# Two-turn attention chunks, paired one-hot tables and contiguous block layout in a graph-network kernel

## The chip, the cores and the metric

The kernel runs on one core of one Trainium2 chip. The metric is device time in microseconds (us), from one launch to its end. A core has five engines that run side by side, each through its own instructions in order: PE (TensorE, the matrix products; its weight loads are listed apart as PEld), DVE (VectorE), ACT (ScalarE), POOL (GpSimd, here almost only the issuer of gathers) and SP (SyncE, here only an issuer of transfers). ACT issues transfers too. All transfers run on 16 shared DMA engines. PE writes to PSUM[...]; a pool of tiles in PSUM or SBUF hands its buffers out in turn, and an instruction that writes a tile waits until the readers of the buffer's last content are done.

## The reference

N = 32768 nodes with D = 128 features, E = 524288 edges sorted by `dst`. Two layers, cut to what matters here:

```python
# layer 0
agg = segment_sum(x[src], dst, N)                       # sum over incoming edges
h = relu((x + agg) @ W_loc1 + b) @ W_loc2 + b;  h_local = bn(x + h)
q, k, v = (x @ Wq, x @ Wk, x @ Wv) as (64 blocks, 512, 8 heads, 16)
attn = softmax(q k^T / 4);  h_attn = bn(x + (attn v) @ Wo)
h = h_local + h_attn;  out0 = bn(h + relu(h @ Wf1) @ Wf2)
x = layernorm(x + out0)
# layer 1, three steps on x
retrieved = softmax((x @ Wq.T) @ keys.T) @ values       # 512 keys
agg = zeros.at[src].add((dinv * x)[dst])                # sum over outgoing edges
x = 0.5 * x + 0.5 * (retrieved - 0.2 * (x - dinv * agg))
# at the end
x = layernorm(x1 + layernorm(x))
```

## The kernel before

The nodes are cut into 64 blocks of 512 (`BLK`), each of four chunks of 128, and into 256 windows of 128 nodes. An edge sum over a window is a chain of 19 matrix products into one PSUM tile (`seg`): each multiplies a 128x128 one-hot matrix (which edge goes to which node of the window) by 128 rows of features. Features travel as three bf16 parts side by side (`ROW` = 384 columns, 768 bytes). Twelve of the 19 row groups come from the regular exchange (`slots`, written by `spread`, read back as `y_i`), five from a list of the window's own leftover edges (`listed`, `OW` = 5), and two from a list that `GW` = 8 windows share (`common`, `SH` = 2). The last seven are gathered row by row from a table in DRAM: POOL issues one `indirect_dma_start` for each 128 rows, in `Exchange.fetch`. So each pass over the 256 windows issues 1280 gathers for `listed` and 64 for `common`.

The one-hot matrices of a window are made by one DVE operation, `Exchange.hot`: 19 x 128 comparisons per partition of a ramp with the column of the table `slot`. The ramp lies in PSUM as 32-bit numbers (`ramp_in_psum`) in two of the passes, and in SBUF as 16-bit numbers (`gc["iota1"]`) in the other two. The value of `slot` is broadcast along the innermost 128 elements.

The program runs in stages, here named by letters with their stretch in the profile:

- **A, 25 to 3529 us:** attention of layer 0, written out by hand in `attention_steps` (an order that the scheduler does not touch), with the preparation of the edge lists ("edge work": sorting networks, shifts and masks, nearly all on DVE) woven in. A *phase* is one block and one parity `o` of the heads (four heads), 128 phases in all; a phase has four chunks. In each chunk PE computes the `scores` of the *next* phase (four heads, two PSUM tiles of two heads each), small extra steps (`early`), and the `weights` products of *this* phase (again two tiles); DVE takes the row maxima of the scores (`maxima`), ACT the exponentials of the weights, and PE multiplies the exponentials of the chunk before by the values (`attend`). At the end of a phase PE transposes the maxima (`lower`), DVE adds them to the queries (`lowered`, tile `ql`, which all `weights` of the next phase read), and `half` or `whole` empties the product. The score and weight tiles come from one pool of three (`at_s`, two banks each).
  The edge work is a generator that yields the cost of what it has issued. `attention_steps` yields a boolean where edge work may be put: at the end of chunks 0 to 2 (True) and after `attend` at the phase's end (False, where work that takes a PSUM bank is not begun). At each such place the loop at the end of the program adds `SHARE` = 3.35 to a quota and issues edge work until the quota is used up.
- **B, 3529 to 4534 us:** `layer0_grid`, first part: rows of `x` are split and spread to `slots`, and the row table is written by `split_steps`.
- **C, 4534 to 6234 us:** `layer0_grid`, second part: the first pass of edge sums, order by hand, gathers asked six windows ahead.
- **D, 6234 to 6490 us:** the feed-forward part.
- **E, 6490 to 7985 us:** `layer1_grid`, first part (pool `l1p`): end of layer 0 and the first spread of layer 1. `load_tables` reads the tables `slot`, `other` and `shared` at its start.
- **F, 7985 to 12472 us:** two passes (`l1w`) in which the edge sums of one step, the retrieval and the spread of the next run together, gathers asked two windows ahead.
- **G, 12472 to 14199 us:** the last pass with the final layer norms (`l1z`), order by hand, gathers asked six windows ahead.

Between the stages, blocks of node rows go through DRAM (`part_d`, `xs_d[0]`, and the row table that the gathers read). `rows_of` writes and reads them as node rows of 128 features: within a partition the four chunks of a block lie 128 rows apart, so each run of a transfer is one row, 512 bytes (768 in the row table).

Of the kernel before, what the change touches and what calls it, by code (L numbers as in the profile page):

```python
# [32 lines left out]
GW = 8  # L33
# [3 lines left out]
SHARE = 3.35  # L37
# [373 lines left out]

class Grid:
# [130 lines left out]
    def build(self, pp):  # L543
# [9 lines left out]
        with tc.tile_pool(name="gr", bufs=1) as sp:  # L553
# [13 lines left out]
            for h in range(2):  # L567
                with tc.tile_pool(name=f"gr_h{h}", bufs=1) as hp:
# [89 lines left out]
                    with tc.tile_pool(name=f"gr_c{h}", bufs=1) as ap:  # L658
# [19 lines left out]
                        for t, n in ((0, 3), (3, OW - 3)):  # L678
# [8 lines left out]
                        nc.vector.tensor_scalar(m, lw, main.oth, P - 1, op0=OP.logical_shift_right,  # L687
                                                op1=OP.bitwise_and)
                        yield two / 3
                        nc.vector.tensor_tensor(m, m, key, OP.bitwise_or)  # L690
                        yield one / 3
# [117 lines left out]
    def build_more(self, lane, pp):  # L809
# [12 lines left out]
        with tc.tile_pool(name="mo", bufs=1) as sp:  # L822
# [10 lines left out]
            for h in range(2):  # L833
# [27 lines left out]
                nc.vector.tensor_scalar(n, word, over.oth, P - 1, op0=OP.logical_shift_right, op1=OP.bitwise_and)  # L861
                yield L / 1000
                nc.vector.tensor_tensor(m, m, n, OP.bitwise_or)
                yield L / 1000
                nc.vector.tensor_tensor(val, m, valid, OP.mult)
# [24 lines left out]
def tile_gnn_resnorm(ctx: ExitStack, tc: tile.TileContext, a: dict, out: bass.AP):  # L890
# [417 lines left out]
    def grid_consts(pool):  # L1308
# [3 lines left out]
        nc.vector.tensor_scalar(gc["lane1"], lane_f, 1.0, None, op0=OP.add)  # L1312
        gc["ident"] = pool.tile([P, P], BF16, name="ident_b")
# [5 lines left out]

    def ramp_in_psum(pool):  # L1320

        t = pool.tile([P, P], F32, name="ramp_p")
        nc.vector.tensor_copy(t, gc["iota1"])
        return t

    class Exchange:
# [16 lines left out]
        def load_tables(self, pool):  # L1343
            self.slot = pool.tile([P, NC2, NW], BF16, name="slot")
            nc.sync.dma_start(self.slot.rearrange("p c w -> p (c w)"), self.grid["slot"])
# [5 lines left out]
        def split_steps(self, wp, b, x, rest):  # L1351
# [7 lines left out]
            def end():  # L1359
                nc.vector.tensor_sub(r[:, :, 2, :], rest, r[:, :, 1, :])  # L1360
                nc.sync.dma_start(rows_of(self.table, b), t)
# [76 lines left out]
        def hot(self, wp, i, ramp, bufs):  # L1438
            oh = wp.tile([P, NC2, P], BF16, name="oh", bufs=bufs)
            nc.vector.tensor_tensor(oh, ramp[:, None, :].to_broadcast([P, NC2, P]),  # L1440
                                    self.slot[:, :, i].unsqueeze(2).to_broadcast([P, NC2, P]), OP.is_equal)
# [54 lines left out]
    def attention_steps(gp, wp, pp, p_pv, p_m):  # L1496
# [79 lines left out]
        def scores(b, o, c):  # L1576
            t = st[b]
            t["two"] = two = [pair(), pair()]
            for s in range(4):
                nc.tensor.matmul(two[s // 2][:, s % 2, :], t["q", o][32 * s:32 * s + 32, c * P:(c + 1) * P],  # L1580
                                 t["k", o][32 * s:32 * s + 32, :], start=True, stop=True)

        def maxima(b, o, c):
            m = mx[o].rearrange("p c (s z) -> p c s z", z=32)
            for i in range(2):
# [88 lines left out]
        def phase(b, o):  # L1674
# [26 lines left out]
            for c in range(NCH):  # L1701
                if n < NB:
                    yield lambda c=c: scores(n, no, c)
# [474 lines left out]
```

## Time and profile before

| | us |
|---|---|
| median of 3 runs | 14195.87 (14195.01 to 14202.4) |
| profiled execution | 14201.3 |
| its span, first to last instruction | 14199.4 |

| engine | busy us | share of the span |
|---|---|---|
| PE | 12173.8 | 86% |
| DVE | 11413.1 | 80% |
| ACT | 6658.1 | 47% |
| POOL | 6079.5 | 43% |
| DMA, all queues | 3603 MB moved | 254 GB/s |

The share over the whole span says little here, because the stages have different limits: POOL issues next to nothing before 4534 us, and the DMA engines are nearly idle during attention. So the reader needs busy time by stage. Among the costliest groups of the page are `listed` (5120 gathers, 1118 ns each on POOL), the one-hot operation (twice 512, at 2681 and 2683 ns on DVE), the row maxima (1024 at 1219 ns on DVE), the exponentials (1024 at 1023 ns on ACT), and the two products of attention: `weights` (L1602) and `scores` (L1580), listed as 4096 instructions each at about 0.7 us, which overlap one another[...].

### The profile page before, as it was taken

What the parts mean: (1) busy time and instruction counts of PE and PEld (TensorE: products, weight loads), DVE (VectorE), ACT (ScalarE), POOL (GpSimd) and SP (SyncE); (2) the same over time, 40 slices, a digit from 0 to 9 for tenths busy, and PEclk for the clock granted to TensorE, in tenths of its full rate; (3) what the DMA queues carried; (4) which work ended last, traced back from release to release, by engine and by line L of the source; (5) the groups of instructions that cost most, each with busy time, mean ns of one, the idle gap of its engine ahead of it and who ended that gap; (6) DMA issues with size and microseconds to landing.
All of it is one profiled execution on the core that took longest, in us unless ns stands there. A gap on an engine that the chain in (4) does not pass through costs nothing. (4 is left out here: it accounts for less than half of the span.)

```text
span 14199.4 us, 168166 instructions
## 1 busy us (share of the span) xinstructions
PE 12173.8 (86%) x58982; PEld 5828.9 (41%) x58982; DVE 11413.1 (80%) x16677; ACT 6658.1 (47%) x10316; POOL 6079.5 (43%) x5461
## 2 busy tenths in 40 slices
PE   8888888889887888888998799999899999966666
PEld 3232223333333444444444355555455555533333
DVE  7998998776998888877888677777677777778888
ACT  4343444334987111127888566666566666610000
POOL 0000000000001777740000477877688878767777
PEclk9898888888999999999999999999999999987787
DMA  1000000000999999977888899999999999988887
GB/s 40 11 11 17 10 11 12 18 8 33 348 346 348 309 309 309 310 242 261 304 311 308 299 383 385 390 383 383 350 376 386 382 391 381 383 292 285 286 283 256
DMA packets 1640075, 3602.99 MB, mean 254 GB/s; under 512 B 199346, under 2 KB 976466, under 8 KB 1638066
## 3 DMA queue, kind: packets, MB, share of 16 engines
q1 hardware_dynamic: 1165424, 2936.81, 55.6%
q0 software_dynamic: 258752, 533.02, 12.3%
q10 hardware_dynamic: 215042, 122.32, 2.8%
q8 instruction: 465, 7.62, 0.2%
q14 instruction: 392, 3.21, 0.1%
HBM read 2088.45 MB, written 1503.00 MB: 253 GB/s over the span
## 5 line engine op out<-in xcount | busy, mean ns | idle before, releaser
L1429 POOL DMA_INDIRECT listed<-rows,other x5120 | 5725.6, 1118 | 3544.2 <-issue 3151.1
L1416 ACT CAST y_o<-exp 128x768 bf16<-128x768 f32 x4224 | 3224.0, 808 | 1271.9 <-DMA slots<-y_o 627.2
L1411 PE MATMUL exp<-rows,pick 128*128 128x384 bf16 x12288 | 2768.2, 326 | 394.9 <-ACT y_o L1416 289.4
L1453 PEld LDWEIGHTS <-oh 128*128 128x128 bf16 x19456 | 1992.2, 102 | 2648.8 <-issue 1629.8
L1453 PE MATMUL seg<-y_i,oh 128*128 128x384 bf16 x12288 | 2745.0, 349 | 9.3 <-DMA y_i<-slots 9.3
L1416 DVE CAST y_o<-exp 128x768 bf16<-128x768 f32 x1920 | 1830.9, 954 | 687.4 <-PE exp L1411 636.2
L1411 PEld LDWEIGHTS <-pick 128*128 128x128 fp8e4 x12288 | 1185.1, 97 | 2115.5 <-issue 1550.7
L1453 PE MATMUL seg<-listed,oh 128*128 128x384 bf16 (+1 forms) x5120 | 1257.6, 336 | 815.5 <-DMA listed<-rows,other 777.2
L1606 ACT ACTIVATE pT<-s 128x1024 f32<-128x1024 f32 x1024 | 1021.5, 1023 | 1353.7 <-PE s L1602 1351.3
L1586 DVE TENSOR_REDUCE mx<-s 128x2 f32<-128x1024 f32 x1024 | 1204.4, 1219 | 270.5 <-PE s L1580 270.2
L1440 DVE TENSOR_TENSOR oh<-ramp_p,slot 128x2432 bf16<-128x2432 f32 x512 | 1372.3, 2681 | 12.7 <-DMA slot<-slot_dst 9.4
L1440 DVE TENSOR_TENSOR oh<-iota,slot 128x2432 bf16<-128x2432 bf16 x512 | 1373.7, 2683 | 3.0 <-DMA slots<-y_o 3.0
L283 POOL DMA_INDIRECT c_r<-pivots_over,c_ix x2 | 1.9, 946 | 3056.7 <-DVE c_ix L281 3056.4
L1602 PE MATMUL s<-ql,k 32*128 32x512 f32 x4096 | 1032.4, 692 | 259.2 <-DVE mx L1586 244.6
L2005 DVE SCALAR_TENSOR_TENSOR part_i<-seg,dinv,part_i 128x128 f32<-128x128 f32 x1536 | 529.6, 345 | 543.0 <-PE seg L1453 531.9
L1064 ACT ACTIVATE ln_rs<-ln_mv,eps_c 128x4 f32<-128x4 f32 x192 | 57.1, 297 | 1670.8 <-DVE ln_mv L1062 1489.7
L1930 PE MATMUL s<-keysT,qT 128*128 128x512 f32 x1536 | 818.2, 615 | 7.3 <-ACT pr L1043 3.7
L1453 PE MATMUL seg<-common,oh 128*128 128x384 bf16 (+1 forms) x2048 | 600.7, 350 | 194.5 <-DMA common<-rows,shared 194.2
L1942 PE MATMUL s<-pt,values 128*128 128x512 f32 x1536 | 750.6, 600 | 10.8 <-ACT pt L1937 10.6
L1580 PE MATMUL s<-k,q 32*128 32x512 f32 x4096 | 745.2, 726 | 6.0 <-DVE mx L1586 2.6
L1613 PE MATMUL pv<-pT,vx 128*32 128x512 f32 x4096 | 698.6, 751 | 0.2 <-ACT pT L1606 0.2
L1388 PE MATMUL row_p<-row,ident_b 128*128 128x512 bf16 x1536 | 601.8, 392 | 82.9 <-DVE pick L1381 62.3
(393 smaller groups left out, 14180.8 us busy)
## 6 DMA issues: line engine op xcount, KB each, us to landing
slots<-y_o SPq DMA_DIRECT2D x2048, 576.0 KB
y_i<-slots SPq DMA_DIRECT2D x1024, 1152.0 KB
pick<-pick SPq DMA_DIRECT2D x1024, 192.0 KB
listed<-rows,other POOLq DMA_INDIRECT x5120
rows<-rows SPq DMA_DIRECT2D x192, 384.0 KB
part_d<-part_o SPq DMA_DIRECT2D x192, 256.0 KB
part_i<-part_d ACTq DMA_DIRECT2D x192, 256.0 KB
rows<-rows SPq DMA_DIRECT2D x64, 386.0 KB
```

The costliest lines, as they stand in the source:

```text
L1411: nc.tensor.matmul(ps[:, j, :ROW], pick[:, o:o + P], r, start=True, stop=True)
L1416: (nc.vector.tensor_copy if to_dve else nc.scalar.copy)(dst, ps[:, :, :ROW])
L1429: nc.gpsimd.indirect_dma_start(out=g[:, k, :], out_offset=None, in_=self.table, in_offset=bass.IndirectOffsetOnAxis(ap=index[:, k:k + 1], ...
L1440: nc.vector.tensor_tensor(oh, ramp[:, None, :].to_broadcast([P, NC2, P]), self.slot[:, :, i].unsqueeze(2).to_broadcast([P, NC2, P]), OP.is ...
L1453: nc.tensor.matmul(ps[:, :n], oh[:, j, :], src, start=(k == 0), stop=(k == NC2 - 1))
L1580: nc.tensor.matmul(two[s // 2][:, s % 2, :], t["q", o][32 * s:32 * s + 32, c * P:(c + 1) * P], t["k", o][32 * s:32 * s + 32, :], start=Tru ...
L1586: nc.vector.tensor_reduce(m[:, c, 2 * i:2 * i + 2, xr[o]], st[b]["two"][i], AX.X, OP.max, negate=True)
L1602: nc.tensor.matmul(two[s // 2][:, s % 2, :], t["k", o][32 * s:32 * s + 32, c * P:(c + 1) * P], t["ql", o][32 * s:32 * s + 32, :], start=Tr ...
L1606: nc.scalar.activation(t["p", c][:, 2 * i:2 * i + 2, :], two[i], AF.Exp)
L1613: nc.tensor.matmul(t["o"][32 * s:32 * s + 32, :], t["v"][:, c, s, 2 * o:2 * o + 2, :].rearrange("p z e -> p (z e)"), t["p", c][:, s, :], s ...
L1930: nc.tensor.matmul(s, st["q"][:, c * P:(c + 1) * P], keysT, start=True, stop=True)
L1942: nc.tensor.matmul(ps, values[:, k, :], st["pt"][:, k, :], start=(k == 0), stop=(k == NCH - 1))
```

## The change

There are six parts.

1. **Attention in two turns a chunk.** `scores`, `maxima` and `weights` get an index `i` and handle two heads and one PSUM tile at a time. A turn issues the `weights` of heads 2i and 2i + 1 and then the `scores` of the other two heads of the next phase. `attend` and the `early` steps follow the first turn. A place for edge work is added after the first turn (`yield False`), so there are eight places in a phase and not four; `SHARE` goes from 3.35 to 1.65, and a yield of −n waits about as many chunks as before.
2. **`GW` from 8 to 16:** sixteen windows share the two common row groups.
3. **`slot` holds each value twice,** window first: the DVE compares pairs of neighbours, so that no operand has an innermost step of 0. `load_tables` reads the table into a temporary tile and makes the two copies on DVE, in C and again in E.
4. **The PSUM ramp** becomes bf16, made by a PE transpose.
5. **Block layout in DRAM:** `kept_of` keeps a partition's four rows next to one another, for the row table, `xs_d[0]` and `part_d`. `x` and `out` keep their layout.
6. **`row_index`:** the gather indices follow the new layout of the row table; it adds four DVE operations to each of the four places where the indices are made.

```diff
-GW = 8
+GW = 16
-SHARE = 3.35
+SHARE = 1.65
+def row_index(nc, dst, spare, window, lane):
+    n = NCH.bit_length() - 1
+    cost = dst.shape[-1] / 1000
+    lane(dst)
+    yield cost
+    nc.vector.tensor_scalar(dst, dst, n, None, op0=OP.logical_shift_left)
+    yield cost
+    nc.vector.tensor_scalar(spare, window, 7, NCH - 1, op0=OP.logical_shift_right, op1=OP.bitwise_and)
+    yield cost
+    nc.vector.tensor_tensor(dst, dst, spare, OP.bitwise_or)
+    yield cost
+    nc.vector.tensor_scalar(spare, window, 7 + n, 7 + n, op0=OP.logical_shift_right, op1=OP.logical_shift_left)
+    yield cost
+    nc.vector.tensor_tensor(dst, dst, spare, OP.bitwise_or)
+    yield cost
...
+    def kept_of(t, i):
+        return t.rearrange("(b p c) d -> b p (c d)", c=NCH, p=P)[i]
...
     def ramp_in_psum(pool):
-        t = pool.tile([P, P], F32, name="ramp_p")
-        nc.vector.tensor_copy(t, gc["iota1"])
+        t = pool.tile([P, P], BF16, name="ramp_p")
+        nc.tensor.transpose(t, gc["down"], gc["ident"])
...
         def load_tables(self, pool):
-            self.slot = pool.tile([P, NC2, NW], BF16, name="slot")
-            nc.sync.dma_start(self.slot.rearrange("p c w -> p (c w)"), self.grid["slot"])
+            self.slot = pool.tile([P, NW, NC2, 2], BF16, name="slot")
+            with tc.tile_pool(name="slot_l", bufs=1) as lp:
+                t = lp.tile([P, NC2, NW], BF16, name="slot_1")
+                nc.sync.dma_start(t.rearrange("p c w -> p (c w)"), self.grid["slot"])
+                for o in range(2):
+                    nc.vector.tensor_copy(self.slot[:, :, :, o], t.rearrange("p c w -> p w c"))
...
         def hot(self, wp, i, ramp, bufs):
-            nc.vector.tensor_tensor(oh, ramp[:, None, :].to_broadcast([P, NC2, P]),
-                                    self.slot[:, :, i].unsqueeze(2).to_broadcast([P, NC2, P]), OP.is_equal)
+            nc.vector.tensor_tensor(oh.rearrange("p c (w z) -> p c w z", z=2),
+                                    ramp.rearrange("p (w z) -> p w z", z=2)[:, None].to_broadcast([P, NC2, P // 2, 2]),
+                                    self.slot[:, i].unsqueeze(2).to_broadcast([P, NC2, P // 2, 2]), OP.is_equal)
...
-        def weights(b, o, c):
-            two = [pair(), pair()]
-            for s in range(4):
-                nc.tensor.matmul(two[s // 2][:, s % 2, :], t["k", o][32 * s:32 * s + 32, c * P:(c + 1) * P],
+        def weights(b, o, c, i):
+            ps = pair()
+            for s in (2 * i, 2 * i + 1):
+                nc.tensor.matmul(ps[:, s % 2, :], t["k", o][32 * s:32 * s + 32, c * P:(c + 1) * P],
                                 t["ql", o][32 * s:32 * s + 32, :], start=True, stop=True)
...
             for c in range(NCH):
-                if n < NB:
-                    yield lambda c=c: scores(n, no, c)
-                yield from early[c]
-                yield lambda c=c: weights(b, o, c)
-                if n < NB:
-                    yield lambda c=c: maxima(n, no, c)
-                if c:
-                    yield lambda c=c: attend(b, o, c - 1)
+                for i in range(2):
+                    yield lambda c=c, i=i: weights(b, o, c, i)
+                    if n < NB:
+                        yield lambda c=c, i=i: scores(n, no, c, 1 - i)
+                    if i == 0:
+                        if c:
+                            yield lambda c=c: attend(b, o, c - 1)
+                        yield from early[c]
+                    if n < NB:
+                        yield lambda c=c, i=i: maxima(n, no, c, 1 - i)
+                    if i == 0:
+                        yield False
                 yield from late[c]
                 if c < NCH - 1:
                     yield True
...
-                nc.sync.dma_start(rows_of(self.table, b), t)
+                nc.sync.dma_start(kept_of(self.table, b), flat(t))
...
-                    nc.sync.dma_start(rows_of(part_d, b), part)
+                    nc.sync.dma_start(kept_of(part_d, b), flat(part))
...
-                    nc.scalar.dma_start(p_i, rows_of(part_d, b))
+                    nc.scalar.dma_start(flat(p_i), kept_of(part_d, b))
...
-                        quota = (us + 1) * SHARE
+                        quota = (2 * us + 1) * SHARE
```

## The prediction

> **What bounds the kernel now.** I read busy time by stage first, because shares of the whole span mix seven different limits. The lines are the stages B, C, D, E, the two passes of F, G and A, each with the busy time of PE, weight loads, DVE, ACT and POOL, then the granted PE clock, the DMA share and GB/s.
>
> ```profile
> core 0: us, PE busy (x) PEld busy (x) DVE busy (x) ACT busy (x) POOL busy (x), PEclk, DMA share, GB/s
> 3529.00:4534.00 1005.00, 839.73 (x3840) 368.34 (x3840) 933.66 (x1289) 895.85 (x1281) 6.57 (x62) 0.99 0.91 344
> 4534.00:6234.00 1700.00, 1374.99 (x6640) 734.75 (x6640) 1497.78 (x2687) 184.73 (x445) 1270.63 (x1344) 0.93 0.93 307
> 6234.00:6490.00 256.00, 242.81 (x528) 96.79 (x528) 143.40 (x209) 135.39 (x197) 0.00 (x0) 0.96 0.59 199
> 6490.00:7985.00 1495.00, 1310.03 (x6025) 693.57 (x6026) 1266.82 (x2375) 1276.27 (x2110) 13.08 (x11) 0.99 0.85 303
> 7985.00:10205.00 2220.00, 2077.22 (x10518) 1137.58 (x10517) 1602.32 (x2094) 1329.16 (x2204) 1736.48 (x1340) 0.99 1.00 376
> 10205.00:12472.00 2267.00, 2117.35 (x10725) 1158.81 (x10722) 1623.37 (x2129) 1373.33 (x2276) 1742.98 (x1339) 0.99 1.00 376
> 12472.00:14199.00 1727.00, 1099.30 (x4864) 546.55 (x4864) 1393.19 (x2881) 39.32 (x129) 1294.97 (x1344) 0.79 0.85 282
> 25.00:3529.00 3504.00, 3108.80 (x15840) 1090.86 (x15839) 2948.37 (x2994) 1420.75 (x1670) 13.78 (x15) 0.87 0.05 15
> ```
>
> F has its DMA engines full (1.00) and PE at 94%. In C and G no engine looks full, yet POOL is. The timeline of POOL, in G and then in F, shows it:
>
> ```profile
> 13200.65 0.94 POOL L1429 DMA_INDIRECT listed<-rows,other  x1 [0.30 <-issue]
> 13201.90 0.94 POOL L1429 DMA_INDIRECT listed<-rows,other  x1 [0.30 <-issue]
> ...
> 9005.42 2.68 DVE L1440 TENSOR_TENSOR oh<-iota,slot 128x2432 bf16<-128x2432 bf16 x1
> 9005.53 3.40 POOL L1429 DMA_INDIRECT listed<-rows,other  x1 [0.30 <-issue]
> ```
>
> In G a gather starts every 1.25 us, 0.94 busy and a constant 0.30 of issue; C's 1344 gathers at 1.25 us are 1680 of its 1700 us. In F the gather that meets a one-hot operation lasts until just after it.
>
> For A I read the waits between 300 and 3000 us (total us, times, longest):
>
> ```profile
> PEld s L1602 <- DVE mx L1586: 422.8, 263, 4.4
> ...
> DVE mx L1586 <- PE s L1580: 147.7, 84, 10.4
> ...
> DVE ql L1596 <- PE m L1591: 54.3, 38, 4.3
> ...
> DVE aval L1628 <- ACT asum L1627: 40.4, 39, 1.8
> ```
>
> The first line is the second pair of weights waiting for a PSUM tile that DVE still reads. The others are DVE's own waits.
>
> The program's own cost yields, summed, give 1485 quota units, which at 3.35 are 443 of the 512 chunks; 69 chunks carry no edge work. Those are PE's: between 3400 and 3500 us PE is busy 98.6 of 100 us with 616 matmul instructions, and at 15840/512 = 30.9 instructions a chunk takes 5.0 us. The others take (3504 - 69 x 5.0)/443 = 7.13 us, 28.5 a phase. DVE works (2948 - 69 x 3.0)/443 = 6.19 us of it, 24.7 a phase (3.0 is its 60% in the free chunks). So DVE bounds A, with 3.8 us of idle a phase; the three DVE waits are 242 us over 2700/28.5 = 95 phases, 2.6 of the 3.8.
>
> [...] the 16-bit one-hot takes 2683 ns, like the 32-bit one. [...] A's clock is 0.87 and the stretch at 3400 us has 1.00.
>
> **The change part by part**, against the execution of 14201.3 us.
>
> *GW.* Each pass issues 32 gathers fewer. In C and G POOL is the limit: 32 x 1.25 = 40 us each, 80 off. I see no second limit within 2%: DVE is busy 88% in C and 81% in G and gets lighter.
>
> *One-hot.* Rows of DVE two-input operations give 1348 ns at 1152 elements and 2547 at 2304, so 1.04 ns per element and 0.15 us fixed; 2432 come to 2.68. [...] 0.15 + 1216 x 1.04 = 1.41 us. It saves 1.27 us of DVE per window, 325 us a pass, but DVE sets the end in none of C, F, G: nothing directly. In F it shortens the hold on POOL, where gathers average 1.28 us against 0.95; POOL is 1736 us busy plus 0.30 x 1340 = 402 of issue, 2138 of 2220, a near second limit that moves out of the way. The PSUM form makes no difference to the sum, as DVE has room.
>
> *Block layout and DMA in F.* A 512-byte packet: the ACT queue in F has 66000 packets at 2.5% of 16 x 4487 us, 27 ns each. A 2 KB packet: in D 24036 packets at 64.8% of 16 x 200 us, 95 ns after setting the 2672 tiny ones at nothing. So four short runs cost 109 ns, one long 95, which makes 4.5 ns of overhead a packet. Part reads, part writes and row writes each drop 3 x 8192 packets a pass: 332 us of engine time, 21 us on 16 engines. Upper value: setting E's and F's SP queue against each other (195 thousand packets, 336 MB, 86% of 16 x 1100 us; 191 thousand, 536 MB, 81.9% of 16 x 1700 us) gives 16 ns a packet for that mix, mostly writes: 62 us with the reads at a middle value. Fewer common rows: 4096 x 36 ns / 16 = 9 us. Between 30 and 71 a pass; I take 45 as the DMA engines are full all along: 90 off for F. If bytes alone count, only the 9 a pass remain. In B, E and G the same saving lies beside DVE, ACT or POOL and counts nothing.
>
> *Table load.* Two DVE copies of 4864 elements, 5.2 us each by the same slope. In C the table is now loaded during B (its transfer stands in the SP queue there), which takes away the 9.4 us for which DVE waited, and POOL runs ahead six windows: nothing. In E the order of instructions shows SP's first load of `pick` waiting for the copies, with the loads of `vT` and `x` behind it on SP; ACT, PE and DVE wait for those. The table needs about 6.9 us to land (as in C), so the first `vT` load goes out at 6490.4 + 6.9 + 10.4 + 0.9 = 6508.6 instead of 6491.8: 16 us on.
>
> *Index.* Four operations more at four places: three at 0.62 and one at 1.09 us (the rows of 896 elements), 12 us of DVE in A.
>
> *Turns in A.* The order of instructions shows weights waiting for DVE (the maxima two turns back) and scores for ACT (the exponentials of the turn before). All of PE's work in a phase at full clock is 4 x (1.14 + 1.14 + 1.06 + about 1.1) + 0.66 = 18.3 us, from the timeline. New on PE: after a chunk's second turn the next scores wait for the exponential just begun: 1.14 + 0.1 + 1.02 us after its weights start instead of 1.14, so 1.1 us, three times a phase; behind them stand `attend` and `early`. At the phase's end `lower` waits for the last maxima (1.3), and the first weights for `lowered` (0.7), with the scores behind. That is 18.3 + 5.3 = 23.6, and 18.3/0.87 + 5.3 = 26.3 at the clock of now. What DVE gains: `lower` no longer stands behind a weights pair and an `attend`, so 2.6 us of waits become about 0.9: 24.7 + 0.9 = 25.6. Two in-order engines that wait for each other end above the larger; I take the middle of 26.3 and 28.5, 27.4 us: 1.1 x 111 phases = 122 off. In chunks without edge work PE is the limit and its path grows from 20.0 to 23.6: 58 such chunks (the yields end at place 908 of 1024), 14.5 phases, 52 on. With 12 for the index: A gives 58 off. Bounds: 26.0 a phase gives 214 off; 30.4 gives 275 on.
>
> Sum: A -58, C -40, G -40, F -90, E +16, B and D 0: -212, so 13989 of 14201.3. The median stands 5.4 under that execution: **13984 us**.
>
> **Rivals.**
> 1. *DVE's idle goes almost wholly.* Phase 26.0: -214 in A, in all -368: 13828. For: most of DVE's idle is at phase ends. Against: PE's path of 26.3.
> 2. *F is limited by bytes.* -18 there: 14056. For: 376 GB/s in both passes, the most of any stage. Against: C and G have 0.93 and 0.85 shares at lower rates, so short packets do cost engine time.
> 3. *Slower: PE becomes the limit of A.* The wait for the exponential, in order, opens gaps[...]. The other parts give 154 off and A's fixed losses are 64, so it decides from (154 - 64)/111 = 0.8 us more a phase, 29.3, which is a mean clock of 18.3/(29.3 - 5.3) = 0.76. At 0.73 the phase is 30.4: A +275, in all +121: 14317. For: stretches of A stand at 0.77 to 0.79 now. Against: ACT is busy 41% in A and answers at once, while now PE waits 423 us for a loaded DVE.
> 4. *The one-hot does not get its double rate.* F keeps POOL near its limit and gets half its gain: about 14030.
>
> **Chances.** Forecast 0.48, rival 1 0.25, rival 2 0.10, rival 4 0.06, rival 3 0.09, other 0.02. A measurement of this kernel tells 0.2% (28 us) from no change. Faster 0.87, same 0.04, slower 0.09. The range, 13770 to 14170, takes in the first two cases with A's bounds, and rivals 2 and 4.
>
> **What would show it.** C and G at about 1660 and 1687 us with 1312 gathers at 1.25 us; `oh` near 1.41 us; F's passes near 2175 and 2220 with gathers near 1.1 us; `vT` of E loaded 16 us later; in A waits of scores on `pT` on PE, fewer DVE waits for `m`, a clock near 0.87 and a length near 3446 us. The prediction is wrong if A's clock falls below 0.76, if gathers in C and G get longer, or if F's DMA stays full at an unchanged length.

## The result and the profile after

The changed kernel takes 14102.55 us (median of 4 runs) where the kernel before takes 14197.09: the ratio is 0.9929, 95% interval 0.9916 to 0.9943. It is faster by 95 us; 212 were forecast, and the predicted time was 13984. The direction was right and the size was less than half.

The stages of the changed kernel, A to G in order, cut at the same events as those shown of the kernel before (columns: stretch, length, then busy time and count of PE, weight loads, DVE, ACT, POOL, then PE clock, DMA share, GB/s):

```profile
25.00:3674.00 3649.00, 2929.18 (x15840) 1063.47 (x15839) 2952.03 (x3010) 1434.22 (x1670) 13.81 (x15) 0.87 0.04 14
3674.00:4676.00 1002.00, 839.20 (x3841) 368.32 (x3841) 933.00 (x1289) 894.25 (x1281) 6.63 (x62) 0.99 0.89 347
4676.00:6342.00 1666.00, 1343.10 (x6645) 719.39 (x6646) 1217.21 (x2691) 185.10 (x445) 1246.83 (x1312) 0.95 0.93 311
6342.00:6600.00 258.00, 242.18 (x525) 95.91 (x523) 143.13 (x206) 135.61 (x197) 0.00 (x0) 0.96 0.58 197
6600.00:8109.00 1509.00, 1313.77 (x6027) 694.90 (x6028) 1273.99 (x2377) 1276.58 (x2110) 12.49 (x13) 0.98 0.83 301
8109.00:10267.00 2158.00, 2067.97 (x10628) 1156.79 (x10627) 1306.03 (x2112) 1352.76 (x2240) 1393.89 (x1328) 0.99 1.01 390
10267.00:12426.00 2159.00, 2068.51 (x10611) 1154.85 (x10610) 1303.76 (x2110) 1352.84 (x2240) 1350.71 (x1283) 0.99 1.01 389
12426.00:14116.00 1690.00, 1090.96 (x4864) 543.61 (x4864) 1074.60 (x2880) 39.32 (x129) 1266.99 (x1312) 0.80 0.84 286
```

| Stage | Before, us | After, us | Change | Forecast |
|---|---|---|---|---|
| A | 3504 | 3649 | +145 | -58 |
| B and D | 1261 | 1260 | -1 | 0 |
| C | 1700 | 1666 | -34 | -40 |
| E | 1495 | 1509 | +14 | +16 |
| F, both passes | 4487 | 4317 | -170 | -90 |
| G | 1727 | 1690 | -37 | -40 |

The forecast is right within 6 us in four rows and wrong in A and F, which err in opposite directions: A is 203 us worse than forecast, F 80 us better. A's clock is 0.87, as before, and DVE is busy for the same time (2952 against 2948 us), so neither a slower clock nor more work explains it. In F the DMA share stays full (1.00, then 1.01) while GB/s rise from 376 to 390: the same bytes cost less engine time.

For A, the waits of the changed kernel between 300 and 3000 us (total us, times, longest):

```profile
PEld m L1623 <- issue: 395.2, 95, 6.8
PE m L1623 <- DVE arec L1674: 306.3, 92, 5.8
...
DVE mx L1618 <- PE s L1613: 239.4, 138, 6.9
PEld s L1613 <- ACT pT L1638: 225.2, 273, 3.8
...
PEld s L1634 <- DVE mx L1618: 177.3, 169, 2.6
PEld s L1634 <- DVE ql L1628: 136.4, 72, 12.0
...
DVE aval L1660 <- ACT asum L1659: 65.0, 45, 1.8
...
DVE ql L1628 <- PE m L1623: 20.8, 27, 1.3
```

The wait of the weights for a PSUM tile that DVE still reads, 423 us before, is down to 177. But DVE's own wait for scores has grown from 148 to 239 us, and PE has waits that are new or far longer: 306 us of `lower` for the reciprocal (`arec`), 136 us of weights for `ql`, 225 us of scores for exponentials (`pT`). The timeline of the changed kernel around the end of one phase shows how they hang together (start, duration, engine, line; in brackets the idle time before and what ended it):

```profile
2019.86 2.35 DVE L1618 TENSOR_REDUCE mx<-s 128x2 f32<-128x1024 f32 x2
2022.12 0.25 DVE L1674 RECIPROCAL arec<-m 128x16 f32<-128x16 f32 x1
2022.29 2.49 DVE L654 TENSOR_TENSOR mask<-kept_w,moved 128x2304 int32<-128x2304 int32 x1
...
2022.52 1.09 PE L1623 MATMUL m<-ident,mx 128*128 128x128 f32 x4 [4.70 <-DVE arec L1674]
...
2024.70 0.68 DVE L1628 TENSOR_TENSOR ql<-m,q 128x512 f32<-128x512 f32 x1
...
2025.43 1.22 PE L1634 MATMUL s<-ql,k 32*128 32x512 f32 x2
...
2027.27 1.23 DVE L1618 TENSOR_REDUCE mx<-s 128x2 f32<-128x1024 f32 x1 [0.37 <-PE s L1613]
...
2041.20 0.30 PEld L1613 LDWEIGHTS s<-k,q 32*128 32x128 f32 x4 [1.35 <-ACT pT L1638]
...
2048.99 0.69 DVE L1628 TENSOR_TENSOR ql<-m,q 128x512 f32<-128x512 f32 x1 [1.27 <-PE m L1623]
...
2052.93 1.23 DVE L1618 TENSOR_REDUCE mx<-s 128x2 f32<-128x1024 f32 x1 [3.25 <-PE s L1613]
```

DVE runs the last two maxima and the reciprocal; PE, whose only other work of the phase (`attend` of the last chunk) stands behind `lower` in its order, stands 4.70 us until `lower` may start. Then DVE takes the edge work of the phase's end (`mask`, 2.49 us) ahead of `ql`. The weights of the new phase wait for `ql`, the first scores come right behind them, and DVE in turn waits for those scores: 0.37 us here, and at the end of the next phase, where no edge work is due, 1.27 us for `lower` ahead of `ql` and 3.25 us for the scores (last two lines). The line at 2041.20 is the other wait that grew: scores held 1.35 us by the exponential of the turn before.

The sizes differ along the stage. Measured from one `ql` to the next, a phase without edge work takes 19.2 to 19.9 us before and 23.9 to 24.0 after. The 82 phases from the eleventh on, called full below, take 27.55 us before and 27.78 after, with DVE busy 24.83 and 24.52 of it. The next 29, called late, go from 29.72 to 31.25 us, with DVE busy 22.8 and 22.9. The first ten and the last six, which carry less edge work or none, are called light.

In F, POOL's timeline of the changed kernel shows the gather that meets a one-hot:

```profile
9006.50 1.45 POOL L1461 DMA_INDIRECT listed<-rows,other  x1 [0.30 <-issue]
```

It lasts 1.45 us in place of the 3.40 of before; the gathers there average 1.05 us (1394 us over 1328).

### The profile page after: what moved, and what is told of

Same layout as the page of the kernel before. It is cut to its first block, busy times and chain, and to the rows that moved or that the text cites. A ratio compares the mean times of both kernels' runs of the same rounds, so it can differ in the third digit from the quotient of the medians.

```text
span 14115.9 us, 167928 instructions
## 1 busy us (share of the span) xinstructions
PE 11898.4 (84%) x58984; PEld 5798.9 (41%) x58984; DVE 10207.9 (72%) x16696; ACT 6674.0 (47%) x10316; POOL 5292.3 (37%) x5333
## 5 line engine op out<-in xcount | busy, mean ns | idle before, releaser
L1461 POOL DMA_INDIRECT listed<-rows,other x5120 | 5146.9, 1005 | 4142.6 <-issue 3147.8
L1486 PE MATMUL seg<-y_i,oh 128*128 128x384 bf16 x12288 | 2636.7, 346 | 21.7 <-DMA y_i<-slots 21.2
L1486 PE MATMUL seg<-listed,oh 128*128 128x384 bf16 (+1 forms) x5120 | 1308.1, 335 | 900.4 <-DMA listed<-rows,other 887.8
L1618 DVE TENSOR_REDUCE mx<-s 128x2 f32<-128x1024 f32 x1024 | 1243.5, 1219 | 448.4 <-PE s L1613 446.6
L1613 PE MATMUL s<-k,q 32*128 32x512 f32 x4096 | 1261.4, 698 | 65.0 <-ACT pT L1638 59.0
L1634 PE MATMUL s<-ql,k 32*128 32x512 f32 x4096 | 1213.0, 683 | 87.0 <-DVE mx L1618 60.2
L1431 DVE TENSOR_SCALAR_CACHE_REDUCE pick<-row_p,lane 128x512 fp8e4<-128x512 f32 x768 | 556.4, 746 | 256.0 <-PE row_p L1420 241.0
L1472 DVE TENSOR_TENSOR oh<-iota,slot 128x2432 bf16<-128x2432 bf16 x512 | 724.1, 1414 | 3.0 <-DMA slots<-y_o 3.0
L1472 DVE TENSOR_TENSOR oh<-ramp_p,slot 128x2432 bf16<-128x2432 bf16 x512 | 723.6, 1414 | 3.5 <-DMA slots<-y_o 3.3
L1486 PE MATMUL seg<-common,oh 128*128 128x384 bf16 (+1 forms) x2048 | 629.2, 349 | 73.4 <-DMA common<-rows,shared 73.2
```

The source lines that it names most:

```text
L1461: nc.gpsimd.indirect_dma_start(out=g[:, k, :], out_offset=None, in_=self.table, in_offset=bass.IndirectOffsetOnAxis(ap=index[:, k:k + 1], ...
L1472: nc.vector.tensor_tensor(oh.rearrange("p c (w z) -> p c w z", z=2), ramp.rearrange("p (w z) -> p w z", z=2)[:, None].to_broadcast([P, NC2 ...
L1486: nc.tensor.matmul(ps[:, :n], oh[:, j, :], src, start=(k == 0), stop=(k == NC2 - 1))
L1613: nc.tensor.matmul(ps[:, s % 2, :], t["q", o][32 * s:32 * s + 32, c * P:(c + 1) * P], t["k", o][32 * s:32 * s + 32, :], start=True, stop=True)
L1618: nc.vector.tensor_reduce(m[:, c, 2 * i:2 * i + 2, xr[o]], st[b].pop(("two", i)), AX.X, OP.max, negate=True)
L1634: nc.tensor.matmul(ps[:, s % 2, :], t["k", o][32 * s:32 * s + 32, c * P:(c + 1) * P], t["ql", o][32 * s:32 * s + 32, :], start=True, stop= ...
```

## The experiments

The kernels ran on different chips. On the one of e1 to e4 and that of e13 the kernel before takes 15095 and 15159 us, on the others 14203 and 14208. On the first of these the stages with gathers are longer (C, F and G of e1 take 1071 us more than those of e6) and A is not: the same order of attention takes 3503 us there (e1) and 3506 on another (e6); for e13's chip there is no such pair. So times are compared only on one chip, and otherwise by stage. The changed kernel itself was timed on neither of the slower chips; e3 below, which leaves its A as it was, takes 0.75% longer than the kernel before on the first, so the gain is not to be expected on every chip. In the text and the tables of this section A is counted to the first cast of the row table, 6 to 8 us more than in the cuts above: 3510 us before, 3657 after.

**e1, the old turns.** Everything of the change except the attention order and SHARE.

```diff
-SHARE = 1.65
+SHARE = 3.35
-                for i in range(2):
-                    yield lambda c=c, i=i: weights(b, o, c, i)
-                    if n < NB:
-                        yield lambda c=c, i=i: scores(n, no, c, 1 - i)
+                if n < NB:
+                    yield lambda c=c: scores(n, no, c)
+                yield from early[c]
+                yield lambda c=c: weights(b, o, c)
...
-                        quota = (2 * us + 1) * SHARE
+                        quota = (us + 1) * SHARE
```

> The changed kernel with the attention order of before (SHARE 3.35, both score tiles first in a chunk); all other parts kept. Theory 1, the two turns themselves cost A's 145 us: stage A goes from 3649 back to about 3510 (3504 plus a few us for the row index), the other stages stay, and the time is 14103 - 139 = about 13964 us (13945 to 13985). Theory 2, A grew for another reason (the index operations, the placing of the edge work around them): A stays above 3600 and the time above 14050.

Measured: A 3503 us, so the two turns, together with the places for edge work and the SHARE that belong to them, are A's whole loss, and the row index costs nothing visible. (e10 below keeps SHARE and the eight places, one of them moved, and has no loss, so their number by itself does not cost it.) The time of 15050.76 (ratio to before 0.9971, 0.996 to 0.9983) missed the expected figure because of the chip, not because of A: C, F and G together are 1071 us longer than in e6, on another chip. Stage C is

```profile
4520.00:6497.00 1977.00, 1453.93 (x6640) 745.22 (x6641) 1189.17 (x2688) 181.94 (x445) 1247.58 (x1312) 0.89 0.80 263
```

which is 311 us more than in the changed kernel above, at a DMA share of 0.80 in place of 0.93. In a run of gathers one still starts every 1.25 us, but 1312 of them make only 1640 of the 1977 us: POOL now also waits, among others 136 us for edge sums (`seg`) where it waited 30 above. Why this chip is slower was not settled.

**e2, extra steps in the second turn.** `early` moves behind the scores of the second turn; `attend` stays in the first.

```diff
-                    if i == 0:
-                        if c:
-                            yield lambda c=c: attend(b, o, c - 1)
-                        yield from early[c]
+                    if i == 0 and c:
+                        yield lambda c=c: attend(b, o, c - 1)
+                    if i == 1:
+                        yield from early[c]
```

> The changed kernel with the extra steps (early) issued in the second turn of a chunk and attend alone left in the first. Theory 1a, PE's wait for the exponential between a second turn and the next chunk's first turn sets the light phases: they fall from 24.0 us towards 21 to 21.5 (three waits of 1.1 us), waits of scores on pT in 300 to 3000 us fall from 267 us to below 120, A loses 60 to 120 us; time 13985 to 14045. Theory 1b, the end and the start of a phase set them (lower behind the last maxima and the reciprocal, scores behind ql): the light phases stay above 23 us and A moves by less than 25 us.

Measured: the first ten phases fall from 25.6 to 22.8 us, the last six from 27.4 to 25.9, the full ones rise from 27.78 to 28.06; A 3623. The waits of scores for exponentials, in all 267 us in the changed kernel (300 to 3000 us), are 139, a little above the 120 expected:

```profile
PEld s L1613 <- ACT pT L1638: 115.0, 109, 3.6
...
PE s L1613 <- ACT pT L1638: 24.1, 60, 2.7
```

The wait for the exponential is real and makes up most of the loss of the first ten phases; it is not what keeps the full ones long. The expected 60 to 120 us were 34, since the full phases gave a part back. The time was 15176.63, ratio 1.0056 (1.0037 to 1.0075).

**e3, scores first at a phase's start.**

```diff
+                    if n < NB and c == i == 0:
+                        yield lambda c=c, i=i: scores(n, no, c, 1 - i)
                     yield lambda c=c, i=i: weights(b, o, c, i)
-                    if n < NB:
+                    if n < NB and (c or i):
                         yield lambda c=c, i=i: scores(n, no, c, 1 - i)
```

> The changed kernel with the scores of the first turn of a phase issued ahead of its weights, the other seven turns unchanged. Theory 1b, DVE stands still at the start of a phase because the scores that it needs stand behind weights that wait for ql: DVE's wait for scores in 300 to 3000 us falls from 239 us to below 150, the full phases (10 to 92) fall from 27.8 us by 0.7 to 1.2, A loses 70 to 130 us; time 13970 to 14035. Theory 1a (the exponential's wait alone): A moves by less than 25 us.

Measured: A 3652, full phases 27.77, and 1.24 us of idle time ahead of the first maxima in place of 1.41; ratio 1.0075 (1.0056 to 1.0095). A miss: DVE's wait for scores was to fall below 150 us and to take 70 to 130 us off A. The scores still stand behind `lower` and `attend`, and at one phase's end in its trace `attend` ends when `ql` is done as well (2029.1 and 2029.0 us), so taking `ql` out of their way is not enough.

**e5, scores ahead of `lower`.** The first scores of the next phase and their maxima are issued before `lower` and `lowered` (`n2` is the phase after the next).

```diff
-                    if n < NB:
+                    if n < NB and c + i:
                         yield lambda c=c, i=i: scores(n, no, c, 1 - i)
...
+            if n2 < NB:
+                yield lambda: scores(n2, no2, 0, 1)
+            yield lambda: attend(b, o, NCH - 1)
             if n < NB:
                 yield lambda: lower(n, no)
-            yield lambda: attend(b, o, NCH - 1)
+            if n2 < NB:
+                yield lambda: maxima(n2, no2, 0, 1)
             yield n == NB
             if n < NB:
                 yield lambda: lowered(n, no)
```

> The changed kernel (two turns) with the first scores of the next phase, and their maxima, issued before the present phase's lower and lowered, and attend of the last chunk ahead of lower; the other seven turns unchanged. Theory 1c, in the full phases DVE stands still at the start of a phase because PE issues nothing for it until lower and attend are through: the idle time ahead of the first maxima falls from 1.4 us a phase to below 0.5, the full phases (10 to 92) from 27.8 to 26.6 to 27.1 us, and A from 3657 to between 3530 and 3590 us. Rival, the idle time only moves on to the next thing that DVE needs (ql, the sum): A stays within 25 us of 3657.

Measured: A 3798, worse by 141, so a miss; 14254.38 us, ratio 1.0038 (1.0024 to 1.0052). Its timeline says why:

```profile
2016.25 2.56 DVE L652 TENSOR_TENSOR moved<-kept_w,mask 128x2304 int32<-128x2304 int32 x1
2018.73 0.68 DVE L1628 TENSOR_TENSOR ql<-m,q 128x512 f32<-128x512 f32 x1
2019.47 0.51 PEld L1634 LDWEIGHTS s<-ql,k 32*128 32x128 f32 x4 [4.44 <-DVE ql L1628]
...
2025.67 1.23 DVE L1618 TENSOR_REDUCE mx<-s 128x2 f32<-128x1024 f32 x1 [6.25 <-PE s L1613]
```

`lower` is done at 2015.3, but DVE has edge work ahead of `ql`, which runs at 2018.73. PE stands for 4.44 us, and since the one set of maxima that was to cover this is already done, DVE then stands for 6.25.

**e9, edge work behind `ql`.** Only the place for edge work at the phase's end moves (here and in e10 and e13 the slot source is kept as in e6, which concerns E alone).

```diff
-            yield n == NB
             if n < NB:
                 yield lambda: lowered(n, no)
             yield lambda: half(b) if o == 0 else whole(b)
+            yield n == NB
```

> The changed kernel (two turns) with the edge work of a phase's end placed behind lowered and half or whole, in place of ahead of them; nothing else in A changed (and the slot source kept, as in e6). Theory 1d: weights first makes PE stand until ql is there, and ql stands on DVE behind that edge work; moved, PE's waits for ql in 300 to 3000 us fall from 154 us to below 60 and the idle time ahead of the first maxima from 1.4 us to below 0.5 a full phase; DVE in turn waits about 1.3 us for lower, so the full phases fall only by 0.3 to 1.0 us, A from 3657 to 3570 to 3630. Rival, the waits for the exponential are all of the loss: A within 20 us of 3657.

Measured: A 3700 (14139.81 us, ratio 0.9955, 0.9939 to 0.9972). The idle time ahead of the first maxima fell from 1.41 to 0.67 and PE's waits for `ql` from 154 to 82 us, neither as far as expected (below 0.5, below 60), and DVE now waits 1.25 us for `lower` ahead of `ql`, where the edge work had covered it: full phases 28.24. A miss in size and sign.

**e10 and e13, the places together.** e13 joins e5 and e9; e10 adds e2's edit.

> e10 with the extra steps left in the first turn as in the changed kernel: e5's scores ahead of lower together with e9's edge work behind ql, slot source kept. Each of these two alone made the full phases longer (29.2 and 28.2 against 27.8 us). Theory 1e, two waits follow one another at the phase's end on DVE (for lower, then for the first products behind ql), and one piece of work covers only one of them: together they bring the full phases below 27.2 us, while the light phases stay above 24 us, since the waits for the exponential remain; A between 3520 and 3580. Rival, moving the extra steps was what helped in e10: the full phases stay above 27.7 us and A above 3620.

> Two turns with e5's scores ahead of lower, e9's edge work behind ql and e2's extra steps in the second turn, slot source kept. If these three places hold the whole loss of the two turns, DVE works nearly through: full phases 26.3 to 26.8 us, light phases 21 to 22.5, A 3420 to 3480, below the 3506 of the old turns. If the turns have a further cost [...], A stays above 3520.

| Kernel | full phases, us | idle of DVE ahead of first maxima / `ql`, us a full phase | first ten phases, us | late phases, us | A, us |
|---|---|---|---|---|---|
| before | 27.55 | 0.51 / 0.53 | 22.2 | 29.7 | 3510 |
| after | 27.78 | 1.41 / 0.24 | 25.6 | 31.3 | 3657 |
| e5 | 29.23 | 2.88 / 0.07 | 24.6 | 32.4 | 3798 |
| e9 | 28.24 | 0.67 / 1.25 | 25.4 | 31.5 | 3700 |
| e13 = e5 + e9 | 27.26 | 0.92 / 0.48 | 24.8 | 30.6 | 3589 |
| e10 = e13 + e2 | 26.77 | 0.34 / 0.68 | 22.7 | 29.5 | 3487 |
| e6, old turns | 27.28 | 0.38 / 0.42 | 22.1 | 29.9 | 3506 |
| e12, old turns, edge moved | 29.60 | 0.05 / 2.65 | 22.3 | 31.5 | 3744 |

e5 and e9, each a loss alone, are together a gain of 68 us: A 3589, just outside the 3520 to 3580 expected, with full phases of 27.26 where below 27.2 was expected (15202.43 us on its chip, ratio 1.0033, 1.002 to 1.0047). Adding e2's edit brings A to 3487, a little above the expected 3420 to 3480. e10 takes 13918.18 us, ratio 0.9797 (0.978 to 0.9813), and is faster than both kernels. Its interval overlaps that of e6 below; that it is ahead of the old turns rests on A, 3487 against 3506 (e1, e6, e7, e8 and e11, all with the old turns' order, have 3503 to 3508). So with its three places mended the order of two turns is worth about 20 us, in one profiled execution. The end of a phase in e10:

```profile
2000.50 1.16 DVE L1617 TENSOR_REDUCE mx<-s 128x2 f32<-128x1024 f32 x1
...
2000.63 0.65 PE L1622 MATMUL m<-ident,mx 128*128 128x128 f32 x4 [1.64 <-DVE arec L1673]
...
2001.57 0.67 DVE L1627 TENSOR_TENSOR ql<-m,q 128x512 f32<-128x512 f32 x1
...
2002.16 1.35 DVE L660 TENSOR_SCALAR mask<-kept_w 128x2304 int32<-128x2304 int32 x1
2002.30 0.31 PEld L1633 LDWEIGHTS s<-ql,k 32*128 32x128 f32 x8 [1.25 <-DVE ql L1627]
...
2004.33 1.23 DVE L1617 TENSOR_REDUCE mx<-s 128x2 f32<-128x1024 f32 x1 [0.82 <-PE s L1612]
```

DVE's two waits of a phase's end each have a piece of work beside them: maxima (1.16 us) beside `lower`, edge work (1.35) beside the first weights. PE waits 1.25 us for `ql`, DVE 0.82 us for the next scores.

**e12, the same move in the old order.** e9's edit on e6.

> e6 (old turns) with the edge work of a phase's end behind lowered, as in e9. In the old order PE has scores to issue that need no ql, so theory 1d says that the place of the edge work matters little: A within 25 us of 3506. If the place matters by itself, A moves by as much as between the changed kernel and e9.

Measured: A 3744, worse by 238 (14178.93 us, ratio 0.9979, 0.9971 to 0.9986). A clear miss of mine: in the old order DVE needs the edge work ahead of `ql`, because `lower` stands on PE behind a pair of weights and an `attend`; without it DVE waits 2.65 us a full phase there. So theory 1d, which looked only at who waits for `ql`, falls; what fits all the cases of the table is 1e: at a phase's end DVE has a wait for `lower` and one for the first scores, and the order decides which of them has work beside it.

**e6, the slot source kept.** With the old turns, the table that the two copies read is taken from the stage's pool and not freed.

```diff
-            with tc.tile_pool(name="slot_l", bufs=1) as lp:
-                t = lp.tile([P, NC2, NW], BF16, name="slot_1")
+            t = pool.tile([P, NC2, NW], BF16, name="slot_1")
```

> Old turns as in e1, and the table that the slot copies read stays allocated, so that the first load of pick in E need not wait for the copies. If E's 14 us are that wait, E goes from 1510 back to 1494 to 1500 us and everything else stays as in e1; if they are the copies themselves on DVE, E stays above 1506. It is also the base for e7 and e8.

Measured, stages A, E and the two passes of F:

```profile
25.00:3523.00 3498.00, 3087.43 (x15840) 1081.12 (x15839) 2958.48 (x3010) 1419.46 (x1670) 13.78 (x15) 0.88 0.05 15
...
6449.00:7944.00 1495.00, 1307.50 (x6025) 692.97 (x6026) 1274.27 (x2377) 1275.65 (x2110) 11.83 (x13) 0.99 0.84 303
7944.00:10104.00 2160.00, 2070.33 (x10626) 1158.49 (x10625) 1303.23 (x2110) 1349.79 (x2238) 1392.60 (x1329) 0.99 1.01 389
10104.00:12252.00 2148.00, 2062.01 (x10616) 1153.61 (x10614) 1304.82 (x2113) 1354.04 (x2243) 1354.53 (x1284) 1.00 1.01 391
```

E is back at 1495 us (1509 in the changed kernel, 1510 in e1): its 14 us were `pick`'s wait for freed memory, and the copies cost nothing else. Time 13943.65, ratio 0.9815 (0.9798 to 0.9831).

**e7, e8, e11 and e4: which part pays in C, F and G.** Each takes one part away from e6: the paired one-hot, with the table copies and the bf16 ramp (e7), GW 16 (e8), the block layout with its index (e11). e8 frees the slot source as the changed kernel does, so its time also holds the 14 us of E; its C, F and G are not touched by that. e4 took the layout away from the changed kernel on the slower chip.

```diff
-                                    self.slot[:, i].unsqueeze(2).to_broadcast([P, NC2, P // 2, 2]), OP.is_equal)
+                                    self.slot[:, :, i].unsqueeze(2).to_broadcast([P, NC2, P]), OP.is_equal)
...
-GW = 16
+GW = 8
-                nc.sync.dma_start(kept_of(self.table, b), flat(t))
+                nc.sync.dma_start(rows_of(self.table, b), t)
...
-                    nc.sync.dma_start(kept_of(part_d, b), flat(part))
+                    nc.sync.dma_start(rows_of(part_d, b), part)
```

> Old turns with the one-hot at single rate (slot table not doubled, 32-bit ramp in PSUM), against e6. Theory 4, the slow one-hot holds POOL's gathers up and F starves for them: F grows by 30 us or more, C and G by less than 10. Theory 3, F is set by its DMA engines alone: F grows by less than 15 us. In both DVE has room in C and G.

> Old turns with GW 8 in place of 16 (32 gathers more a pass), against e6. If POOL's 1.25 us a gather sets C and G, each grows by 35 to 42 us and F by 8 to 15 a pass; if on this chip the landing of gathers sets them, C and G grow by less than 20.

> e6 (old turns, slot source kept) with the node-row layout of before and no row index. On a chip where the DMA engines are full in F, as in the runs before and after, theory 3 (12 to 16 ns a packet) gives F + 110 to 150 us against 4302; theory 4 less than 80. C, G, B and E within 10 us.

> The changed kernel with the node-row layout of before in DRAM (runs of 512 and 768 bytes) and without the row index; GW, one-hot and turns kept. Theory 3, the cost of a packet was taken too small (4.5 to 12 ns; 73728 packets a pass at 16 ns are 74 us on 16 engines): F grows from 4317 us by 130 to 150, A loses 0 to 12, time about 14225 to 14255. Theory 4, a good part of F's 170 us comes from POOL, whose gathers the faster one-hot no longer holds up: F grows by less than 100 us and the time stays below 14200.

The two passes of F without the paired one-hot (e7), then without the block layout (e11):

```profile
7939.00:10124.00 2185.00, 2085.29 (x10629) 1146.72 (x10628) 1613.49 (x2111) 1351.57 (x2240) 1731.50 (x1330) 0.99 1.00 385
10124.00:12301.00 2177.00, 2078.98 (x10611) 1143.50 (x10609) 1610.50 (x2112) 1350.97 (x2241) 1692.32 (x1283) 0.99 1.01 386
```

```profile
7952.00:10186.00 2234.00, 2086.33 (x10626) 1155.39 (x10624) 1308.98 (x2111) 1349.54 (x2240) 1391.13 (x1328) 0.99 1.01 376
10186.00:12420.00 2234.00, 2081.66 (x10613) 1152.50 (x10612) 1306.98 (x2111) 1351.03 (x2241) 1345.45 (x1283) 0.99 1.01 376
```

C and G in e6, then in e8:

```profile
4520.00:6194.00 1674.00, 1351.66 (x6649) 721.69 (x6649) 1220.00 (x2693) 186.34 (x447) 1250.23 (x1312) 0.95 0.93 311
...
12252.00:13941.00 1689.00, 1091.41 (x4864) 543.97 (x4864) 1075.12 (x2880) 39.32 (x129) 1266.78 (x1312) 0.80 0.85 286
```

```profile
4525.00:6233.00 1708.00, 1383.51 (x6650) 738.34 (x6649) 1215.27 (x2693) 186.25 (x448) 1273.66 (x1344) 0.93 0.92 306
...
12298.00:14028.00 1730.00, 1092.94 (x4864) 543.19 (x4864) 1075.09 (x2881) 39.32 (x129) 1295.07 (x1344) 0.79 0.84 281
```

Against e6's 2160 and 2148 us, e7's passes are 25 and 29 longer: 54 us for the one-hot. POOL is busy 1731 us of 2185 there, plus 0.30 us of issue for each of its 1330 gathers, 2130 in all: near the end of the pass, as before the change. Over both passes it waits 62 us there for edge sums to free a gather's tile, and 692 in e6, so its slack is nearly gone. The DMA engines are full in both (shares of 1.00 and 1.01), so how the two limits share the 54 us is not shown. e7's C and G are within 10 us of e6's. e11's are 74 and 86 longer, 160 us for the layout, at 376 GB/s, the rate of before; 110 to 150 were expected. e8's passes are 9 us shorter in sum, no more than F differs between e6 (4308) and the changed kernel (4317), so GW shows no gain in F, where 8 to 15 us a pass were expected; C and G grow by 34 and 41 us (to 1708 and 1730), POOL's 32 gathers. The parts of F sum to more than the 179 us between before and e6, as they may, since each was removed with the others in place. The times: e7 13997.03 (0.9855, 0.9839 to 0.9872), e8 14014.38 (0.9862, 0.9845 to 0.9878), e11 14129.36 (0.9947, 0.993 to 0.9963). e4's F, 4895 us on the slower chip, is only 36 to 69 longer than in e1, e2 and e3 (4826 to 4859): there the DMA share in F is 0.96 and the layout counts less. (Its A is 24 us below that of the changed kernel; e11's is 2 below e6's, so this is not put down to the index.) Its time, 15228.82 (1.0085, 1.0069 to 1.0102), does not tell theories 3 and 4 apart for the chip of the result; e7 and e11 do: both parts pay, and of theory 3's 16 ns a packet only the total comes near (below).

The DMA queue that SP fills, over F, first in e11, then in e6 (packets, MB, share of 16 engines):

```profile
q1 hardware_dynamic: 494131, 1388.02, 80.9%
```

```profile
q1 hardware_dynamic: 395941, 1387.92, 81.8%
```

On queue 1, 98190 packets fewer save 0.809 x 16 x 4468 - 0.818 x 16 x 4308 = 1451 us of engine time. It would be wrong to divide the one by the other (14.8 ns each), because most of the queue's packets are the same in both. Sorted by size, the packets of the two traces took, in us of all 16 engines together:

| Packets in F | e11 | e6 |
|---|---|---|
| writes of `part_d`, 512 bytes or 2 KB | 112 (27.4 ns each) | 86 (84.6 ns each) |
| writes of the row table, 768 bytes or 3 KB | 148 (36.1 ns) | 125 (121.8 ns) |
| reads of `part_d`, 512 bytes or 2 KB | 109 (27.4 ns) | 87 (87.2 ns) |
| the rest of SP's queue, mostly 4608 bytes, unchanged | 3354 (187.4 ns at 4608 bytes) | 3314 (185.2 ns) |
| gathers, unchanged | 756 | 732 |

The packets that the layout changed save 71 us, about 8 ns for each packet that is gone, writes and reads alike. Another 65 us lie in packets that it did not change and that became a little shorter. The stretch is 160 us shorter; the last 24 were not settled, nor why the unchanged packets became shorter.

## Why the prediction was wrong

- **C and G, right.** 80 us forecast, 71 measured, with 1312 gathers still at 1.25 us. e8 gives the gain back, 75 us.
- **One-hot, right in its duration, wrong in its worth.** 1.41 us was forecast and 1.414 measured, with the ramp in PSUM (1414 ns) and in SBUF (1415 ns) alike. That pairs would halve the 1.04 ns per element of the trace was the author's estimate, which nothing in the kernel before showed. "Nothing directly" was wrong: POOL, "a near second limit that moves out of the way", was given no price, and e7 shows 54 us for the one-hot in F.
- **Layout, mis-sized.** Of the 45 us a pass 36 were for the layout, 72 for both, between the lower value of "4.5 ns of overhead a packet" and the upper one of 16. The packets that the layout changed did save 71. That the middle came out so is chance: the 95 ns of a 2 KB packet, read in D, were 84.6 to 87.2 in F, so the lower value should have been 7 to 8 ns, and the upper one had its 16 ns from a mix of packets, while those on SP's queue cost no more than those on ACT's (27.4 ns each at 512 bytes). The step that failed is that the layout saves these packets' own time and nothing else: e11 shows 160 us for it. Packets of unchanged size became shorter too, 65 us, which no term of the sum had; the last 24 are open.
- **GW in F, wrong.** 18 us were forecast for fewer common rows; e8 shows no gain.
- **Table load, right.** +16 forecast, +14 measured; e6 shows the mechanism, memory freed after the copies (E 1495 us where it is kept).
- **Index, too dear.** 12 us forecast in A; with it A is 3506 us in e6 and without it 3504 in e11.
- **A, wrong in sign.** PE's side held: clock 0.87, path of a phase without edge work 23.6 us forecast and 24.0 measured, waits for the exponential where they were expected. The step that failed is DVE's, "2.6 us of waits become about 0.9". Between 300 and 3000 us the three waits counted there were 242 us before and are 325 after (239 for scores, 65 for `aval`, 21 for `lower`), 3.4 us over each of the same 95 phases. The part that was argued came true, the wait for `lower` fell; but I priced the wait of the first weights for `lowered` at 0.7 us, the duration of that operation, and left out the edge work standing ahead of it on DVE, and DVE's own wait for the scores that now stand behind those weights. e9 shows that moving the edge work alone does not help; e13 and e10 show that covering both waits does. In the full phases the gain of 1.1 us became a loss of 0.23, in the late ones a loss of 1.53: 82 x 0.23 + 29 x 1.53 = 63 us in place of -122. The light phases cost 33 us in the first ten and 47 in the last six, 80 against 52 forecast; edge work now reaches into the last six (DVE busy 17.4 us a phase, 11.9 before).
- **The mean behind A's sum.** 28.5 us a phase with 3.8 us of DVE idle mixes two kinds of phase. The full ones had 2.7 us of idle before, the late ones 6.9. In the late ones DVE's wait for scores was 83 us over the 29 phases before and is 160 after, and 60 us before were steps of the sorting networks (`more_a`, `more_b`) waiting for PE and ACT. The forecast of 1.1 us a phase was less than either idle time, so the mean alone does not explain the sign.
- **Rivals.** The slower one had A's sign but put it down to a lower clock, a link that was the author's assumption; the clock stayed at 0.87. The first one asked for 26.0 us a phase, 1.5 of the 2.7 us of idle in the full ones; in this order DVE's waits grew, and even e10 has 26.77. The second falls with e11: with short packets F took 160 us more at equal bytes. The fourth falls with the 1.41 us of the one-hot.

The measured time lies inside the range of 13770 to 14170, near its upper end, but by luck: without the 80 us that F gave beyond its forecast it would lie above it.

## What to carry to other kernels

Before pricing a new wait at the duration of the awaited instruction, look at what stands ahead of that instruction on its own engine, and at who waits in turn for the engine that waits. An engine's idle time found as a mean over a stage should be split by kind of iteration before it is multiplied by all of them. A cost read in one stage may not hold in another: a 2 KB packet took 95 ns in D and 85 in F. A queue's total divided by the packets that went is not their cost while other packets share the queue. Where two in-order engines hand work back and forth at a loop's boundary, count the waits in one round and give each its own piece of independent work: here two moves that lost 141 and 43 us alone gained 68 together.

## What the runs showed of the hardware

- The one-hot compare of 2432 elements, all inputs 16-bit and the slot values in equal pairs, took 1414 ns with the ramp in PSUM and 1415 with it in SBUF. With single slot values it took 2681 (a 32-bit ramp in PSUM) and 2683 (a 16-bit ramp in SBUF).
- A packet of 512 bytes took 27.4 ns in F (e11) and one of 2 KB 84.6 (writes) or 87.2 (reads) in e6: four short ones cost 8.3 or 7.4 ns more for each of the three that go, so writes and reads about alike.
- The kernel before takes 14197 to 14208 us on some chips and 15095 and 15159 on two others, 6 to 7% more. Between e6 and e1, which differ only in whether the slot source is freed, 1071 of the 1085 us lie in the stages with gathers: C 1674 and 1977 us, F 4308 and 4826, G 1689 and 1939, with gathers of a run starting every 1.25 us in both.
